# A Mamba block and an FFN on one core: the first stage rebuilt, with TensorE on zeros, softplus in PSUM and masked products for x

## The chip, the cores and the metric

The kernel runs on one core of one Trainium2 chip. A core has a matrix engine (TensorE, PE in the profile; its weight loads are shown as PEld), three elementwise engines (VectorE or DVE, ScalarE or ACT, GpSimd or POOL) and a queue engine (SyncE or SP) that only issues transfers here. They run side by side and wait for one another by semaphores. SBUF is the on-chip memory of 128 partitions; PSUM, also of 128 partitions, receives what TensorE produces, and VectorE and ScalarE can read and write it, too.

The metric is the device time of one execution in microseconds; lower is better. The kernel before has a median of 599.46 us over 3 runs, from 594.8 to 600.17.

## What is computed

Four images of 512 tokens by 256 channels. Everything is float32. A layer norm with a shift and scale per image, an SSM-like attention (Mamba-2 form) with 32 heads of width 8 and state 64, a gated residual, a second layer norm, and an FFN whose hidden layer passes through a Walsh-Hadamard transform:

```python
h = layernorm(x) * (1 + ca) + sa
proj = h @ W_in.T
xBC, z, A_log = split(proj, [4352, 4608])
xBC = causal_conv4(xBC, conv_w) + conv_b
x_, Bm, Cm = split(xBC, [256, 256 + 32 * 64])
a = -softplus(A_log)
Lm = exp(segsum(a))
M = einsum("blhn,bshn,bhls->bhls", Cm, Bm, Lm)
y = einsum("bhls,bshp->blhp", M, x_) + D * x_
x = x + ga * ((y * silu(z + z_bias)) @ W_out.T)
h = layernorm(x) * (1 + cb) + sb
x = x + gb * (fwht(silu(h @ W1.T) * (h @ W3.T)) @ W2.T)
```

The shifts, scales and gates (sa, ca, ga, ...) are slices of silu(c) @ wmod.

## The kernel before

**Tiling.** Eight units, (i, b): i is a half of the heads (16), b an image. A unit has eight pairs of heads, numbered k = 0 to 63 over all units. For a pair, `project` makes the B part (`pbc`, half 0) and the C part (`pcc`, half 1) in PSUM, each with six matmuls (L245): weights and activations are kept as a high and a low float32r half (`split` makes those of the weights: a rounding copy on ScalarE or VectorE, and a subtract on GpSimd), and three of the four products are summed over two halves of the 256 channels. `conv` then applies the four-tap convolution: two operations on ScalarE (L387, L389), two on VectorE (L390, L391) and one on GpSimd (L392). `prep_l` makes the decay matrix of a pair with one bfloat16 matmul of two prepared constants, `dls` and `drs`, into which `load_d` writes the sums of this image from DRAM. `attend` does B times C for two pairs and multiplies with the decays; `turn_b`, `states`, `turn_states`, `intra` and `inter` do the chunked scan of the states, in chunks of 64 tokens.

**The prologue of an image**, in five parts: `normalize` (part 0), `modulate` (part 1: eight transposes into `pt`, then `ht`, the activations in two halves, and `full`), softplus and running sums (part 2: `pa`, abs, exp, ln, max, subtract, scan; then the sums in three bfloat16 `parts`, which go to DRAM in the tiles `p`, `pd` and `pend`), the decays to a chunk's end (part 3) and their transpose `wdec` (part 4).

**The x stage of a unit**: `x_proj` and `conv` give x; `x_part2` copies each chunk twice; `x_part3` transposes it, puts x of each head into its own columns of `xpad` (zero elsewhere), and x times the decays into `xwz` (zero elsewhere).

**Order.** Each piece is traced at a time on an agenda (`at_time`; one unit of time is one pair), with the times in the dict `T`. From that, a planner with its own model of the durations orders the instructions of TensorE, VectorE, ScalarE and GpSimd; only SP's queue keeps the order as written. `behind(engine)` makes an instruction follow a given one on its own engine's queue, without a wait. `AHEAD` is the number of pairs projected before the agenda starts. The start of image 0 is written out by hand (L651 to L688). On PSUM, `m` and `p` are pools of three buffers each.

Of the kernel before, what the change touches and what calls it, by code (L numbers as in the profile page):

```python
# [30 lines left out]
def mamba_ffn(tc, ctx, u, c_t, wmod, win_t, cw, cb, zb, dsk, wo_t, w13_t, w2_t,  # L31
# [50 lines left out]
    ac.activation(warm, neghalf, AF.Tanh)  # L82
    c_sb = cload(c_t.rearrange("(k p) b -> p k b", p=128), [128, 2, NB], "c_sb")
# [15 lines left out]
    wms = {}  # L99
    for grp in (0, 1):  # L100
        load_mod(grp, nc.sync, "bt", 6)
# [45 lines left out]
    xwz = const.tile([128, 4, 4, 2, 2, 16], F32, name="xwz")  # L147
    for t in (xpad, xwz):
        gp.memset(t, 0.0)
# [7 lines left out]
    for t in dls:  # L157
        ac.activation(t, kdl.unsqueeze(1).to_broadcast([94, 8, 128]), AF.Copy)
    for t in drs:
        ac.activation(t, kdr.unsqueeze(1).to_broadcast([94, 4, S]), AF.Copy)  # L160
# [9 lines left out]
    def split(dst, c0, width, ts, e=ac):  # L170

        for k, t in enumerate(ts):
# [5 lines left out]
            gp.tensor_tensor(d[:, 1], t, d[:, 0].bitcast(F32), ALU.subtract)  # L178

    wa = const.tile([128, 2, 32], F32, name="wa")  # L180
    nc.sync.dma_start(wa, win_t[:, 512:544].rearrange("(k p) c -> p k c", p=128))
# [4 lines left out]
    def fetch_quad(n, half, **kw):  # L186
        return fetch(win_t[:, 544 + 1024 * n : 544 + 1024 * n + 1024], 512 * half, 512, f"wq{n}", **kw)

    def split_quad(n, half, ts, e=ac):
        if half == 0:  # L190
            wq[n] = work([128, 2, 2, 1024], f"wq{n}", "wq", 2, F32R)
        split(wq[n], 512 * half, 512, ts, e)
# [4 lines left out]
    def fetch_xz(i, **kw):  # L197
        return fetch(win_t[:, 256 * i : 256 * i + 256], 0, 256, f"wxz{i}", **kw)

    def split_xz(i, ts, e=ac):  # L200
        wxz[i] = work([128, 2, 2, 256], f"wxz{i}", "wxz", 1, F32R)
        split(wxz[i], 0, 256, ts, e)
# [44 lines left out]
    last = {}  # L247

# [10 lines left out]

    def behind(*engines):  # L260
        stack = ExitStack()
        for e in engines:
            stack.enter_context(tc.issue_after(last[e].ins))
        return stack
# [21 lines left out]
    def modulate(b, which, xn):  # L286
# [4 lines left out]
        for t in range(4):  # L291
            for k in range(2):
                pe.transpose(pts[k][:, 128 * t : 128 * t + 128], xn[:, t, 128 * k : 128 * k + 128], ident)  # L293
# [30 lines left out]
    def prologue(b, part, fill=None):  # L324
# [9 lines left out]
        elif part == 2:  # L334
# [8 lines left out]
            at = work([128, 128], f"at{b}", "at", 1)  # L343
            ac.activation(e, pa, AF.Abs)
            last[ve] = ve.tensor_scalar(at, pa, 0.0, -1.0, ALU.max, ALU.mult)
# [4 lines left out]
            ve.tensor_tensor(at, at, e, ALU.subtract)  # L350
            phs = phss[b] = work([128, 128], f"phs{b}", "phs", 1)
            ve.tensor_tensor_scan(phs, reset, at, 0.0, ALU.mult, ALU.add)
# [538 lines left out]
```

## Time and profile before

The profile is of one execution of 600.72 us, whose instructions span 598.8 us; the median of the runs is 599.46 us.

| | us |
|---|---|
| span of the profiled execution | 598.8 |
| its time | 600.72 |
| TensorE busy (matmuls) | 550.4 |
| VectorE busy | 419.3 |
| ScalarE busy | 389.5 |
| GpSimd busy | 329.0 |
| first matmul starts | 7.63 |
| first B part (pbc of pair 0) starts | 15.62 |
| first decay matmul (pl) starts | 28.15 |
| first `xpad` copy, unit 0 | 59.20 |
| first `xpad` copy, unit 1 | 110.71 |
| first `xpad` copy, unit 7 | 427.86 |

Lines of the profile give, for a group, the source line, the engine, the operation, the tile written and those read (with buffer numbers left out), shapes, and the count. In the order of time, the first number is the start, the second the duration, both in us; the bracket at the end is the idle time of that engine before it, and whose end released it. A table by stage has the width first, then the busy time of PE, PEld, DVE, ACT and POOL with the number of instructions, the granted share of the TensorE clock, the DMA engines' busy share, and GB/s.

### The profile page before, as it was taken

The numbers are of one execution on the slowest core, as the hardware profiler recorded it, in microseconds if no ns is written. First come the engines' busy times: TensorE is split into PE (matmuls) and PEld (weight loads), VectorE is DVE, ScalarE is ACT, GpSimd is POOL, SyncE is SP. The second block draws the span as 40 slices with busy tenths as digits, with TensorE's granted clock in tenths as the row PEclk, the third lists the DMA queues.
The fourth block names the chain that finished last, engine by engine and source line by source line (L and its number), as shares of the span: only waits on it lengthen the run. The fifth ranks groups of instructions, "written<-read, shape, count | busy, mean of one in ns | idle before, by whom it ended". The sixth has DMA issues, their size and how long they took to land. (4 is left out here: it accounts for less than half of the span.)

```text
span 598.8 us, 16340 instructions
## 1 busy us (share of the span) xinstructions
PE 550.4 (92%) x6836; PEld 436.1 (73%) x6836; DVE 419.3 (70%) x763; ACT 389.5 (65%) x650; POOL 329.0 (55%) x302
## 2 busy tenths in 40 slices
PE   3798999799899989999999898899989999999996
PEld 3565676577577766767777676667768888888886
DVE  5957987987887785889787778789875354343242
ACT  5879688688956878886794787577774333322321
POOL 5673447255635577556465647466577546334341
PEclk9988999999999999999999799989999999999999
DMA  6323111021122343023103143145138035204021
GB/s 195 117 66 143 36 36 72 21 59 70 42 56 73 112 147 112 3 60 117 59 4 111 67 105 113 58 128 184 38 121 292 22 105 167 99 1 150 1 79 36
DMA packets 42113, 52.00 MB, mean 87 GB/s; under 512 B 18230, under 2 KB 30260, under 8 KB 42040
## 3 DMA queue, kind: packets, MB, share of 16 engines
q1 hardware_dynamic: 40504, 50.54, 26.6%
q8 instruction: 54, 0.88, 0.6%
q10 hardware_dynamic: 1472, 0.38, 0.3%
q14 instruction: 19, 0.16, 0.1%
q0 software_dynamic: 64, 0.05, 0.0%
HBM read 33.51 MB, written 17.44 MB: 85 GB/s over the span
## 5 line engine op out<-in xcount | busy, mean ns | idle before, releaser
L392 POOL TENSOR_TENSOR cc<-cc,cv 128x509 f32<-128x509 f32 x64 | 70.0, 1094 | 70.3 <-DVE cc L391 58.3
L392 POOL TENSOR_TENSOR bc<-bc,cv 128x509 f32<-128x509 f32 x64 | 69.9, 1092 | 56.3 <-DVE bc L391 28.3
L245 PE MATMUL f<-h,wf 128*128 128x512 f32 x384 | 97.2, 394 | 0.0
L245 PEld LDWEIGHTS f<-h,wf 128*128 128x128 f32 x384 | 68.8, 189 | 12.3
L390 DVE SCALAR_TENSOR_TENSOR cc<-pcc,cw_sb,cc 128x511 f32<-128x511 f32 x64 | 47.6, 744 | 35.2 <-ACT cv L389 35.2
L706 POOL TENSOR_TENSOR fl<-ft,fh 128x512 fp32r<-128x512 f32 x31 | 40.0, 1293 | 56.8 <-ACT fh L705 52.2
L387 ACT ACTIVATE bc<-pbc,cb_sb,cw_sb 128x512 f32<-128x512 f32 x64 | 50.0, 781 | 21.1 <-PE pG L258 15.7
L387 ACT ACTIVATE cc<-pcc,cb_sb,cw_sb 128x512 f32<-128x512 f32 x64 | 50.2, 784 | 19.9 <-PE pcc L245 14.8
L245 PE MATMUL pcc<-ht,wq 128*128 128x512 f32 x192 | 55.8, 426 | 7.1 <-DVE dx L489 3.0
L705 ACT ACTIVATE fh<-ft 128x512 fp32r<-128x512 f32 x32 | 20.2, 631 | 58.7 <-DVE ft L702 28.9
L701 DVE SCALAR_TENSOR_TENSOR ft<-ft,f 128x512 f32<-128x512 f32 x32 | 21.9, 687 | 51.3 <-ACT ft L700 51.2
L245 PE MATMUL pbc<-ht,wq 128*128 128x512 f32 x192 | 55.6, 426 | 0.5 <-ACT bt L466 0.5
L245 PE MATMUL pcc<-hr,wq 128*128 128x512 f32 x192 | 54.1, 417 | 1.4 <-DVE bc L391 0.7
L245 PE MATMUL pbc<-hr,wq 128*128 128x512 f32 x192 | 52.0, 405 | 3.3 <-DVE cc L391 3.2
L390 DVE SCALAR_TENSOR_TENSOR bc<-pbc,cw_sb,bc 128x511 f32<-128x511 f32 x64 | 47.5, 743 | 10.7 <-ACT cv L389 10.4
L245 PEld LDWEIGHTS pcc<-ht,wq 128*128 128x128 f32 x192 | 36.9, 201 | 17.0 <-ACT cv L389 3.7
L391 DVE SCALAR_TENSOR_TENSOR bc<-pbc,cw_sb,bc 128x510 f32<-128x510 f32 x64 | 47.6, 743 | 1.3
L391 DVE SCALAR_TENSOR_TENSOR cc<-pcc,cw_sb,cc 128x510 f32<-128x510 f32 x64 | 47.5, 742 | 1.2
L466 ACT ACTIVATE bt<-bT 128x512 f32<-128x512 f32 x64 | 38.7, 605 | 10.8 <-PE bT L464 10.7
L245 PEld LDWEIGHTS pbc<-ht,wq 128*128 128x128 f32 x192 | 37.0, 201 | 10.4 <-ACT bt L466 0.9
L258 PEld LDWEIGHTS pG<-cc,bc 64*64 64x64 f32 x2048 | 34.5, 135 | 13.5 <-issue 7.9
L389 ACT ACTIVATE cv<-pbc,cw_sb 128x512 f32<-128x512 f32 x64 | 44.2, 691 | 0.0
(153 smaller groups left out, 1256.8 us busy)
## 6 DMA issues: line engine op xcount, KB each, us to landing
wq<-win_t SPq DMA_DIRECT2D x16, 256.0 KB
htd<-ht SPq DMA_DIRECT2D x8, 512.0 KB
hr<-htd SPq DMA_DIRECT2D x8, 512.0 KB
h2d<-ht SPq DMA_DIRECT2D x8, 512.0 KB
h<-h2d SPq DMA_DIRECT2D x8, 512.0 KB
x<-u SPq DMA_DIRECT2D x7, 512.0 KB
ex<-pd SPq DMA_DIRECT2D x8, 256.0 KB
ygd<-yg SPq DMA_DIRECT2D x4, 512.0 KB
```

Source lines behind the costliest of these rows:

```text
L245: last[pe] = pe.matmul(ps, w[:, a, k, c0 : c0 + 128], ht[k][:, b], start=(n == 0), stop=(n == 5))
L258: self.before = pe.matmul(*args, **kw)
L387: ac.activation(dst, ps, AF.Identity, bias=cb_sb[:, tl : tl + 1], scale=w[:, 3:4])
L389: last[ac] = ac.activation(v, ps, AF.Copy, scale=w[:, 0:1])
L390: ve.scalar_tensor_tensor(dst[:, 1:], ps[:, : S - 1], w[:, 2:3], dst[:, 1:], ALU.mult, ALU.add)
L391: last["conv"] = ve.scalar_tensor_tensor(dst[:, 2:], ps[:, : S - 2], w[:, 1:2], dst[:, 2:], ALU.mult, ALU.add)
L392: last[gp] = gp.tensor_tensor(dst[:, 3:], dst[:, 3:], v[:, : S - 3], ALU.add)
L466: ac.activation(bts[k], pt, AF.Copy)
L701: ve.scalar_tensor_tensor(t, t, 1.0, p1, ALU.add, ALU.mult)
L705: ac.activation(hi, t, AF.Copy)
L706: (ve if (b, f) == (NB - 1, 7) else gp).tensor_tensor(lo, t, hi.bitcast(F32), ALU.subtract)
```

## The change

- TensorE gets 22 matmuls of zeros at its start and 9 more behind the transposes of image 0.
- The weights that the first stage needs come in one transfer for both halves of the channels instead of two, before the prologue of image 0, into buffers of `ht`; so do the first two groups of `wmod`, into a buffer of `yg`.
- The copies of the constants `dls` and `drs` are halved: the second set is made at time 2.6 of the agenda, behind the last conv then traced on ScalarE.
- `q00` (the weights of pairs 0 and 1) is split after `modulate` of image 0; the low halves of the next weights are made in a given order.
- Softplus: max and add in one operation that writes PSUM in place, and a scan that reads it from there and subtracts.
- The three parts go to DRAM in one transfer (before: four, two of them from GpSimd for image 0), `pd` too.
- Three pairs instead of two are projected before the agenda.
- `xpad` is written by one product with the 0/1 mask `own` for each half of the tokens (before: four copies of 64 partitions), `xwz` by two products of 128 partitions with decays that are zero where they have to be (before: four of 64 partitions). `xwz` has a new layout, `wdec` holds a masked copy for each of two chunks, and `xwz` needs no zeroing any more.
- `dx`'s first column is zeroed on ScalarE instead of VectorE.

```diff
+    def keep_warm(n):
+        for _ in range(n):
+            last[pe] = pe.matmul(warm_ps, idle[:, :128], idle, start=True, stop=True)
+
+    keep_warm(22)
...
+    wm01 = work([128, 2, 2 * DM], "wm01", "yg", 1)
+    nc.sync.dma_start(wm01, wmod[:, : 2 * DM].rearrange("(k p) c -> p k c", p=128))
     for grp in (0, 1):
-        load_mod(grp, nc.sync, "bt", 6)
+        wms[grp] = wm01[:, :, DM * grp : DM * grp + DM]
...
-    for t in (xpad, xwz):
+    for t in (xpad, *sts):
         gp.memset(t, 0.0)
...
-    for t in dls:
-        ac.activation(t, kdl.unsqueeze(1).to_broadcast([94, 8, 128]), AF.Copy)
-    for t in drs:
-        ac.activation(t, kdr.unsqueeze(1).to_broadcast([94, 4, S]), AF.Copy)
+    def spread_constants(n, *engines):
+        with behind(*engines):
+            ac.activation(dls[n], kdl.unsqueeze(1).to_broadcast([94, 8, 128]), AF.Copy)
+            ac.activation(drs[n][:88], kdr[:88].unsqueeze(1).to_broadcast([88, 4, S]), AF.Copy)
+
+    spread_constants(0)
...
+    def fetch_both(src, c0, width, name, tag, bufs):
+        t = work([128, 2, width], f"{name}_{c0}", tag, bufs)
+        nc.sync.dma_start(t, src[:, c0 : c0 + width].rearrange("(k p) c -> p k c", p=128))
+        return [t[:, 0], t[:, 1]]
...
-            last[ve] = ve.tensor_scalar(at, pa, 0.0, -1.0, ALU.max, ALU.mult)
...
-            ve.tensor_tensor(at, at, e, ALU.subtract)
+            ve.scalar_tensor_tensor(pa, pa, 0.0, e, ALU.max, ALU.add)
             phs = phss[b] = work([128, 128], f"phs{b}", "phs", 1)
-            ve.tensor_tensor_scan(phs, reset, at, 0.0, ALU.mult, ALU.add)
+            ve.tensor_tensor_scan(phs, reset, pa, 0.0, ALU.mult, ALU.subtract)
...
-            for t in range(4):
-                (gp if T["p3gp"] and b == 0 and t % 2 else nc.sync).dma_start(p_dr3[b][:, :, 128 * t : 128 * t + 128], parts[32 * t : 32 * t + 32])
+            nc.sync.dma_start(p_dr3[b].rearrange("h r (t l) -> t h r l", t=4), parts)
...
-            wdec[b] = const.tile([128, 4, NH], F32, name=f"wd{b}")
-            ac.activation(wdec[b].rearrange("p t h -> p (t h)"), pw, AF.Copy)
+            wdec[b] = const.tile([128, 4, 2, NH], F32, name=f"wd{b}")
+            for q in range(2):
+                ac.activation(wdec[b][:, :, q], pw.rearrange("p (t h) -> p t h", h=NH), AF.Copy,
+                              scale=own[:, 0, 8 * q : 8 * q + 1])
 
     def write_sums(b, phs):
+        nc.sync.dma_start(p_dr[b].rearrange("h (t l) -> t h l", t=4), phs)
         for t in range(4):
-            nc.sync.dma_start(p_dr[b][:, 128 * t : 128 * t + 128], phs[32 * t : 32 * t + 32])
...
-    AHEAD = 2
+    AHEAD = 3
...
-        ve.memset(de[:, :, 0:1], 0.0)
+        ac.activation(de[:, :, 0:1], de[:, :, 0:1], AF.Copy, scale=0.0)
...
+            v = xpad[:, :, 4 * hf : 4 * hf + 4, :, :16].rearrange("p a c g x -> p a (c g) x")
+            v = bass.AP(v.tensor, v.offset, [v.ap[0], [v.ap[1][0] + 16, 2], *v.ap[2:]])
+            ve.tensor_tensor(v, pt.rearrange("p c (g a x) -> p a (c g) x", g=4, a=2),
+                             own[:, 0].unsqueeze(1).unsqueeze(1).to_broadcast([128, 2, 16, 16]), ALU.mult)
+            for t in range(2):
+                ve.tensor_tensor(xwz[:, 2 * hf + t].rearrange("p h q x -> p q h x"),
+                                 pt[:, 2 * t : 2 * t + 2].rearrange("p q (h x) -> p q h x", x=8),
+                                 wdec[b][:, 2 * hf + t, :, 16 * i : 16 * i + 16]
+                                 .unsqueeze(3).to_broadcast([128, 2, 16, 8]), ALU.mult)
...
-    early = dict(tag="cc", bufs=8)
-    prologue(0, 0)
+    early = dict(get=fetch_both, tag="ht", bufs=6)
     q00 = fetch_quad(0, 0, **early)
-    fxz = fetch_xz(0, **early)
+    nc.sync.dma_start(wa, win_t[:, 512:544].rearrange("(k p) c -> p k c", p=128))
+    fxz = fetch_xz(0, get=fetch_both, tag="cc", bufs=8)
     q01 = fetch_quad(0, 1, **early)
     q10 = fetch_quad(1, 0, **early)
-    q11 = fetch_quad(1, 1)
+    q11 = fetch_quad(1, 1, **early)
+    prologue(0, 0)
+    prologue(0, 1)
+    with behind(ve):
+        split_quad(0, 0, q00, ve)
+    with behind(pe):
+        keep_warm(9)
     with behind(gp):
-        split_quad(0, 0, q00, ve)
-    prologue(0, 1)
-    with behind(gp):
-        for t in sts:
-            gp.memset(t, 0.0)
         gp.tensor_scalar(hzb, zb_sb, 0.5, None, ALU.mult)
...
-            split_xz(0, fxz, ve)
-            split_quad(0, 1, q01, ve)
+            split_xz(0, fxz, ve, True)
+            split_quad(0, 1, q01, ve, True)
+
+            lows.insert(0, lows.pop())
+            for n in range(4):
+                with behind(*[gp] * (n > 0)):
+                    last[gp] = gp.tensor_tensor(*lows.pop(0))
...
-    prologue(0, 3)
+    with behind(ac):
+        prologue(0, 3)
...
+    at_time(2.6, spread_constants, 1, ac)
```

## The prediction

> **What bounds the kernel now.** I read the page first, for shares.
>
> ```profile
> span 598.8 us, 16340 instructions
> PE 550.4 (92%) x6836; PEld 436.1 (73%) x6836; DVE 419.3 (70%) x763; ACT 389.5 (65%) x650; POOL 329.0 (55%) x302
> ```
>
> TensorE leaves 48 us idle in the whole span. A change to the first stage can win that stage's part of the 48 us, plus the time in which TensorE works at half clock. The table by stage shows how much that is:
>
> ```profile
> 0.00:10.00 10.00, 2.37 (x12) 2.40 (x12) 4.26 (x12) 5.15 (x6) 6.42 (x14) 1.00 0.58 165
> 20.00:30.00 10.00, 6.85 (x28) 5.13 (x27) 9.72 (x17) 9.47 (x16) 7.14 (x8) 0.87 0.13 26
> 30.00:45.00 15.00, 13.74 (x115) 9.83 (x113) 8.52 (x20) 11.46 (x21) 10.72 (x10) 0.86 0.22 69
> 75.00:105.00 30.00, 28.96 (x515) 22.52 (x514) 23.87 (x36) 26.63 (x46) 18.31 (x17) 1.00 0.14 54
> ```
>
> (The columns are PE, PEld, DVE, ACT, POOL, granted clock, DMA share, GB/s.) By 75 us TensorE has idled 16.7 us (the stages' busy times summed); from 75 to 105 us it is 97% busy. So time won at the start should be carried on, as far as the other engines follow. The order of time says who sets the start:
>
> ```profile
> 7.63 3.55 PE L111 MATMUL pm<-sc,wm 128*128 128x4 f32 x16 [7.63 <-DMA wm<-wmod]
> 15.62 2.93 PE L245 MATMUL pbc<-ht,wq 128*128 128x512 f32 x6
> 20.72 1.55 PE L245 MATMUL pbc<-ht,wq 128*128 128x512 f32 x6
> 28.15 1.01 PE L428 MATMUL pl<-dr,dl 94*128 94x512 bf16 x2 [3.15 <-DMA dr<-p]
> 29.67 2.91 PE L245 MATMUL pbc<-ht,wq 128*128 128x512 f32 x6
> ```
>
> The same six matmuls take 2.93, 1.55 and 2.91 us. The clock row grants about half at 28 to 34 us; at 15 us it says 1.00, but 0.49 us each is the half-clock pace, so I read it as cold. Then the softplus chain, DVE and POOL:
>
> ```profile
> 18.44 1.37 DVE L350 TENSOR_TENSOR at<-at,spe 128x128 f32<-128x128 f32 x1
> 19.84 1.38 DVE L352 TENSOR_TENSOR_SCAN phs<-reset,at 128x128 f32<-128x128 f32 x1
> 18.20 2.75 POOL L178 TENSOR_TENSOR wq<-wq,wq 128x512 fp32r<-128x512 f32 x2
> 53.89 0.29 DVE L350 TENSOR_TENSOR at<-at,spe 128x128 f32<-128x128 f32 x1 [1.27 <-ACT spe L349]
> ```
>
> With GpSimd busy the subtract takes 1.37 us, ending 0.24 us after GpSimd's own; for image 1, with GpSimd idle, 0.29 us (the scan 0.42). Last, one x stage:
>
> ```profile
> 108.61 1.25 PE L513 MATMUL xt<-ident,xd 128*128 128x128 f32 x8 [1.22 <-DVE l L458]
> 110.71 1.20 DVE L518 COPY xpad<-xt 64x128 f32<-64x128 f32 x4
> 111.92 1.00 DVE L526 TENSOR_TENSOR xwz<-xt,wd 64x128 f32<-64x128 f32 x4
> ```
>
> VectorE has 6.73 us of work in the 7 us from 109 to 116 while TensorE has 5.46: here VectorE decides.
>
> **The change, part by part** (against the profiled execution: span 598.8 us, time 600.72 us, so 1.9 us outside; the median of the runs is 599.46, 1.3 below).
>
> *Warm start.* pm (3.55 us), pt and the first projections run cold. The 22 zeros have no row; their streaming length is the projections', 0.49 us cold and 0.26 warm. TensorE warmed between 14.6 us and about 20.5 (in pcc of pair 0: 2.54 us is about 4.7 slow and 1.3 fast), 5.9 us: 12 cold and 10 warm, 8.5 us from about 1.0. Then pm starts at 9.5 instead of 7.63 and takes half, 1.75: 11.25 against 11.18. If it warms sooner, pm ends at 10. The xn chain ends at 10.50 (unmoved: x halves, rs on GpSimd 1.04 us, four normalises 2.65), so pt ends at 11 to 11.7, not 12.98: 1.3 to 2.0 us won, I take 1.7. The Trainium skill (TensorE: Matmul & The Clock Gate, "What's actually happening") puts the warm-up at about 3.4 us of sustained work in a free-running window; by that, pm would end near 10 and this step win 2.0; the sum below, which goes by a later row, stays.
>
> *Moved split.* Today q00's casts and GpSimd subtracts lie at 10.4 to 14.1, under waits. Now they stand behind the last ht subtract (15.87, less 1.7: 14.2). Casts 2 x 0.43, subtracts 2 x 1.27: low halves exist at about 17.2, and pbc of pair 0, which needs the second low for its fourth term, ends at about 18.0 against 18.55. So only 0.5 of the 1.7 us reaches the first projection, and TensorE half idles for 3 us (the nine zeros lie before it), which can cool it (worth up to 1.4 us on the first pair, a row apart). GpSimd then runs the four lows of wxz and q01 (4.35 us) to 21.5, against 20.95.
>
> *Softplus in PSUM, one p write.* L345 (0.28) goes; the subtract and scan read one operand from PSUM. Without the waits 1.37 and 1.38 become 0.29 and 0.42: 2.0 us. But the four parts operations and df now lie under GpSimd's lows, and those with two SBUF operands can each wait out one, as L350 did (1.1 us each). Net 0.5 to 3.5 us, I take 1.5: parts at 21 instead of 22.47. Four DMAs on two queues (22.50 to 25.45 until dl could issue) become one of SP: one issue 0.66 and the 1.9 us that POOL's queue shows to landing, 2.6 against 2.95. The first pl comes at 26 instead of 28.15. The GPSIMD Engine Reference (1. Specifications) says that GpSimd shares its SBUF interfaces with VectorE, in contention with VectorE instructions of two SBUF inputs or a two-port mode. Row and rule agree that PSUM frees the scan; the same rule speaks against the change at parts and casts, and if by it the chain won nothing and TensorE waited for that, the sum below would be -7.0.
>
> *Third pair ahead.* Pair 2's projections fill 25.0 to 28.15, which was idle (3.15), and run warm: 2.91 + 2.37 - 2 x 1.55 = 2.2. TensorE has done the same work at about 28.5 instead of 34.75: 6.2 us at most. GpSimd, though, has 7 conv adds x 1.09 and 4 lows x 1.26 after 21.5: 34.2 at best for image 1's rs, today at 35.44; VectorE's nm, today 1.15 us late behind a conv (37.63), then comes at once: xn starts near 36.4, not 38.72, 2.3 us. Image 1's pt stands on TensorE around attend(1). So the start gains between 1.2 and 6.2; I take 3.0, near the xn row.
>
> *Constants in two halves.* Today 5.9 us of copies lie in ScalarE's early idle time. The second half, 1.05 + 1.90, moves to time 2.6, that is about 40 us, where ScalarE is busy 11.40 of 12 us (38 to 50) and the pl of pair 4 waits for it. Cost 0 (ScalarE has 4.8 of 15 us free from 60 on) to 2.95: I take 1.5.
>
> *Masked products.* Per half 1.20 + 1.00 = 2.2 us. New: one 128x512 product from PSUM, 0.68 (the row of ot<-po,gate), and two of 256 columns, 0.42 (fo<-pdy,gate): 1.52, less some overlap. About 0.75 saved per half, 12 us of VectorE over 8 units. TensorE idles 1.54 us from 109 to 116, so not all can come back; I take one half's worth per unit, 8 x 0.75 = 6 (bounds 0 and 12).
>
> *Softplus of images 1 to 3.* 0.28 each, and 0.88 and 1.40 instead of 0.29 and 0.42 for images 2 and 3: 4 us of VectorE just before an x stage; half: 2.
>
> *ScalarE extras.* dx's zeroing moves from a 0.07 us memset to ScalarE, 8 x 0.2 (th's row); wd gets a second 0.28, four times: 2.8 us, ScalarE busy 82% in the units: 1 (0 to 2.8).
>
> *At nothing:* the larger loads: all five weight loads and wa now pass SP before image 1's x, wa behind q00 (q00 landed by 12.3, now used at 14; x, wm and q00, 1.5 MB, at the 275 GB/s of 2 to 6 us need 5.5 us; cover some 4 us; wa is wanted at about 13); df's exp, put behind pair 2's and x's convs on ScalarE (some 30 instead of 21.7; pw used it at 34.4; without that cover pw holds TensorE by what is missing); five write_sums DMAs for eight, GpSimd's memsets (2.6 us before 4.45, sts 1.63 for xwz 0.95), states reading xwz in the other layout, 32 columns as before. ScalarE, VectorE, GpSimd and TensorE are ordered anew by the planner from its own model, with no row: either sign, some 3 us.
>
> Sum: -3.0 + 1.5 - 6 - 2 + 1 = -8.5: 600.72 - 8.5 = 592.2, some 591 by the median. I say **592**.
>
> **The rivals.**
> *Wider gain, 585 (22%).* TensorE's own 6.2 us is carried, and the x stage gives 1.2 us a unit: -6.2 + 1.5 - 9.6 - 2 + 1 = -15. For it: TensorE at 97% in 75 to 105. Against it: GpSimd's 12.7 us before rs.
> *Nothing visible, 597.5 (16%).* GpSimd keeps rs where it was (gain 1.2), the constants take 1.5 back, and TensorE, 95% busy between x stages (42.71 of 45 us), absorbs most of VectorE's relief, leaving 3. For it: TensorE's 92%.
> *ScalarE becomes the bound, 605 (17%).* 2.95 + 1.6 + 1.1 = 5.7 us is added to ScalarE on its path, and late convs hold the PSUM buffers that projections want; already TensorE stood still for 2.5 us before pcc at 46.42, while convs were late. It decides if ScalarE's idle time per unit is less than what TensorE saves, so VectorE's relief shows up as VectorE waiting for cv. Against it: cv waits today cost VectorE 46 us in all, but little of the chain. 600.7 + 5.7 - 1.2 = 605.
> *Zeros that do not warm* would be 22 x 0.49 = 10.8 us: pm ends at 15.3, 4 us late, and the start gains nothing (contained in the two cases above).
>
> **How the numbers follow.** A measurement of this kernel tells about 1% (6 us) from no change. The forecast, 45%, spreads over 588 to 597; three quarters of it lie under 593.5 (0.34). Faster: 0.34 + 0.22 = 0.56. Within 1%: 0.11 + 0.16 = 0.27. Slower: 0.17. Range 584 to 603: it leaves out about a third of the wide gain and half of the slow case, under 2 in 10, and takes in both ends of the constants and x stage.
>
> **What would show it.** Right: pm from about 9 us in under 2 us; L350's successor at 0.3 us and the scan at 0.42 beside a busy GpSimd; six-matmul projections at 1.55 us throughout 18 to 28; no 3 us gap before the first pl; xpad plus xwz at 1.4 us a half; the second x stage before 106 us (110.71 today). Wrong: parts operations over 1 us, rs of image 1 after 35, TensorE idle for cv near 45, or an order in the units that leaves x stages later.

## The result and the profile after

The changed kernel takes **603.03 us** (median of 20 runs, 598.62 to 606.6); the kernel before, run beside it, 598.03 (20 runs, 594.8 to 601.72). The ratio is 1.0077, with a 95% interval of 1.005 to 1.0104: slower by 0.8%. The prediction said 592, between 584 and 603. The profiled execution took 601.07 us, 2 us less than its median.

First the shares, from the page of the changed kernel:

```profile
span 599.3 us, 16282 instructions
PE 553.3 (92%) x6867; PEld 434.6 (73%) x6867; DVE 403.5 (67%) x672; ACT 391.2 (65%) x662; POOL 325.9 (54%) x299
```

VectorE lost 15.8 us of work (419.3 before), and the span did not follow. The table by stage of the changed kernel (width, then PE, PEld, DVE, ACT, POOL busy, granted clock, DMA share, GB/s) shows where TensorE lost time instead. The second table is the kernel before in the stages from 45 to 75 us:

```profile
20.00:30.00 10.00, 7.73 (x34) 6.11 (x33) 9.76 (x14) 8.40 (x14) 6.93 (x8) 0.99 0.13 27
30.00:45.00 15.00, 11.15 (x109) 7.96 (x108) 8.06 (x19) 12.72 (x23) 10.31 (x10) 0.89 0.18 48
45.00:60.00 15.00, 10.89 (x114) 7.78 (x112) 8.65 (x18) 14.91 (x25) 5.58 (x6) 0.89 0.37 150
60.00:75.00 15.00, 13.16 (x199) 10.14 (x200) 11.85 (x27) 8.57 (x17) 5.37 (x5) 0.77 0.19 41
```

```profile
45.00:60.00 15.00, 12.49 (x123) 8.98 (x123) 10.96 (x24) 14.12 (x25) 5.83 (x6) 0.89 0.36 140
60.00:75.00 15.00, 14.48 (x215) 10.34 (x213) 13.84 (x36) 10.18 (x19) 6.62 (x6) 1.00 0.18 36
```

From 20 to 30 us it has what was forecast, a warm and busier TensorE (7.73 us for 6.85). From 30 to 75 TensorE is busy for 35.20 us, where before it was 40.71 (13.74 + 12.49 + 14.48), and part of that at a low clock: 0.77 in the last 15 us, 1.00 before. In the order of time, on TensorE of the changed kernel:

```profile
1.17 7.55 PE L98 MATMUL warm<-idle 128*128 128x512 bf16 x22 [1.17 <-DVE idle L93]
8.56 1.84 PE L131 MATMUL pm<-sc,wm 128*128 128x4 f32 x16
...
17.71 1.65 PE L280 MATMUL pbc<-ht,wq 128*128 128x512 f32 x3 [0.32 <-POOL wq L214]
19.16 2.03 PE L280 MATMUL pcc<-ht,wq 128*128 128x512 f32 x6
...
28.89 1.62 PE L280 MATMUL px<-ht,wxz 128*128 128x512 f32 x6 [2.27 <-DVE cc L419]
30.36 0.61 PE L456 MATMUL pl<-dr,dl 94*128 94x512 bf16 x2
...
39.96 0.44 PE L320 MATMUL pt<-ident,xn 128*128 128x128 f32 x2 [3.37 <-ACT xn L310]
...
42.05 1.97 PE L291 MATMUL pG<-cc,bc 64*64 64x64 f32 x60
...
47.67 2.90 PE L280 MATMUL pcc<-ht,wq 128*128 128x512 f32 x6 [2.31 <-ACT dl L180]
```

The zeros warm TensorE: pm takes 1.84 us (3.55 before) and pt starts at 10.26. The gain is then spent: the first projection ends at 19.36 (18.55 before); px waits 2.27 us for a conv, so the gap before the first pl has only moved; TensorE waits 3.37 us for the normalised image 1 before its transposes; and at 45 us it stands still for 2.31 us, as it did for 2.48 before, and works on at half pace. The first decay product on VectorE, at L486, comes at 43.89 us (42.76 before): the rebuilt first stage is 1.1 us later at its end, not 3 us earlier. About half of that is the later start of the transposes (39.96 us for 39.37), and the rest the half clock behind the wait: the 60 matmuls of `pG` take 1.97 us, where they took 1.15. VectorE and GpSimd between:

```profile
18.40 0.28 DVE L376 SCALAR_TENSOR_TENSOR pa<-pa,spe 128x128 f32<-128x128 f32 x1
18.72 0.42 DVE L378 TENSOR_TENSOR_SCAN phs<-reset,pa 128x128 f32<-128x128 f32 x1
19.18 0.74 DVE L382 CAST parts<-phs 128x128 bf16<-128x128 f32 x1
19.84 0.83 DVE L396 TENSOR_TENSOR df<-phs 128x128 f32<-128x128 f32 x1
20.60 0.82 DVE L383 TENSOR_TENSOR rest<-phs,parts 128x128 f32<-128x128 f32 x1
21.45 1.20 DVE L384 CAST parts<-rest 128x128 bf16<-128x128 f32 x1
```

```profile
18.56 1.27 POOL L701 TENSOR_TENSOR wq<-wq,wq 128x512 fp32r<-128x512 f32 x1 [0.38 <-DVE wq L207]
19.79 1.48 POOL L701 TENSOR_TENSOR wxz<-wxz,wxz 128x256 fp32r<-128x256 f32 x2
21.23 1.33 POOL L701 TENSOR_TENSOR wq<-wq,wq 128x512 fp32r<-128x512 f32 x1
...
35.58 2.51 POOL L214 TENSOR_TENSOR wq<-wq,wq 128x512 fp32r<-128x512 f32 x2
38.04 1.03 POOL L302 TENSOR_TENSOR rs<-rs,neghalf 128x4 f32<-128x4 f32 x1
```

Max-and-add takes 0.28 and the scan 0.42 us beside a busy GpSimd, as forecast. But the four operations after them now take 0.74, 0.83, 0.82 and 1.20 us. In the kernel before they took 0.23 to 0.29, two of them in these lines:

```profile
21.26 0.23 DVE L356 CAST parts<-phs 128x128 bf16<-128x128 f32 x1
21.40 0.29 DVE L371 TENSOR_TENSOR df<-phs 128x128 f32<-128x128 f32 x1
```

In the changed kernel all four end with the GpSimd subtracts beside them, as the subtract and the scan did before. The wait went from the scan to its successors, and the parts are done at 22.98 us (22.47 before). The GPSIMD Engine Reference of the Trainium skill (1. Specifications) gives the conditions, two SBUF inputs or a two-port mode of VectorE; these rows agree, and the casts, with one SBUF input, would be of the second kind, which no run here separates.

The x stage is as forecast, a half of it in the time of VectorE's first two rows:

```profile
62.62 0.68 DVE L545 TENSOR_TENSOR xpad<-xt,own 128x512 f32<-128x512 f32 x1
63.22 0.74 DVE L548 TENSOR_TENSOR xwz<-xt,wd 128x256 f32<-128x256 f32 x2
```

1.4 us for 2.2 us. But the first of them starts at 62.62 instead of 59.20, and the second unit's at 117.89 instead of 110.71.

### The profile page after: what moved, and what is told of

It reads as the page before. It is cut to its first block, busy times and chain, and to the rows that moved or that the text cites. A ratio compares the mean times of both kernels' runs of the same rounds, so it can differ in the third digit from the quotient of the medians.

```text
span 599.3 us, 16282 instructions
## 1 busy us (share of the span) xinstructions
PE 553.3 (92%) x6867; PEld 434.6 (73%) x6867; DVE 403.5 (67%) x672; ACT 391.2 (65%) x662; POOL 325.9 (54%) x299
## 4 chain that ended last, share of the span: by engine, by line
PE 59%; ACT 15%; DVE 12%; DMA 6%; issue 3%; POOL 2%; SPq 0%; ACTq 0%; POOLq 0%; DVEq 0%
PE f L280 13%; PE pcc L280 10%; PE pbc L280 7%; PE pdyi L745 4%; PE pdy L745 4%; PE pG L291 4%; ACT cv L417 3%; PE py L574 3%; PE bT L492 3%; PE ps L558 2%; PE po L638 2%; ACT bc L415 2%; PE pz L280 2%; ACT xn L310 2%; DVE cc L418 2%
## 5 line engine op out<-in xcount | busy, mean ns | idle before, releaser
L418 DVE SCALAR_TENSOR_TENSOR cc<-pcc,cw_sb,cc 128x511 f32<-128x511 f32 x64 | 47.5, 743 | 32.4 <-ACT cv L417 32.4
L280 PE MATMUL pcc<-ht,wq 128*128 128x512 f32 x192 | 58.1, 441 | 7.9 <-DVE bc L419 2.9
L418 DVE SCALAR_TENSOR_TENSOR bc<-pbc,cw_sb,bc 128x511 f32<-128x511 f32 x64 | 47.5, 742 | 14.1 <-ACT cv L417 14.0
L280 PE MATMUL pbc<-ht,wq 128*128 128x512 f32 x192 | 53.9, 412 | 2.3 <-POOL wq L214 1.2
L280 PEld LDWEIGHTS pcc<-ht,wq 128*128 128x128 f32 x192 | 38.1, 208 | 20.5 <-DVE bc L419 5.3
L419 DVE SCALAR_TENSOR_TENSOR bc<-pbc,cw_sb,bc 128x510 f32<-128x510 f32 x64 | 47.5, 742 | 1.3
L419 DVE SCALAR_TENSOR_TENSOR cc<-pcc,cw_sb,cc 128x510 f32<-128x510 f32 x64 | 47.5, 742 | 1.1
L486 DVE TENSOR_TENSOR l<-pG,l 128x512 f32<-128x512 f32 x64 | 41.0, 682 | 10.5 <-PE pG L291 6.6
L492 PE MATMUL bT<-ident,bc 128*128 128x128 f32 x256 | 41.2, 283 | 4.2 <-ACT bt L494 2.9
L417 ACT ACTIVATE cv<-pcc,cw_sb 128x512 f32<-128x512 f32 x64 | 44.2, 690 | 1.0 <-POOL bc L420 1.0
```

Of the source, the lines that this page charges most:

```text
L280: last[pe] = pe.matmul(ps, w[:, a, k, c0 : c0 + 128], ht[k][:, b], start=(n == 0), stop=(n == 5))
L417: last[ac] = ac.activation(v, ps, AF.Copy, scale=w[:, 0:1])
L418: ve.scalar_tensor_tensor(dst[:, 1:], ps[:, : S - 1], w[:, 2:3], dst[:, 1:], ALU.mult, ALU.add)
L419: last["conv"] = ve.scalar_tensor_tensor(dst[:, 2:], ps[:, : S - 2], w[:, 1:2], dst[:, 2:], ALU.mult, ALU.add)
L486: ve.tensor_tensor(lts[n], pg, lts[n], ALU.mult)
L492: pe.transpose(pt[:, t], bc[:, 128 * t : 128 * t + 128], ident)
```

## The experiments

The theory after the trace: the masked products win what they should, and three other parts take it back, namely the constants' second half at 46 us on ScalarE, the third pair ahead (its conv adds stand before image 1's rs on GpSimd) and the late split of `q00`. The rival: the change is a loss because the masked products gain nothing, or because the order of the units is worse throughout. All were run in 3 rounds beside the kernel before; a ratio is to that, with its interval. Landmarks are from the profiled executions: "decay product n" is the start of VectorE's multiplication of `pG` by the decays for pair n. Each is one execution, up to 5.6 us away from its kernel's median (591.01 for 596.64 us in the one furthest off), so landmarks tell where a loss lies, and medians how large it is.

**The masked products, alone on the kernel before, and taken out of the changed kernel.**

```diff
-            for pp in range(2):
-                for j in range(2):
...
+            ve.tensor_tensor(v, pt.rearrange("p c (g a x) -> p a (c g) x", g=4, a=2),
+                             own[:, 0].unsqueeze(1).unsqueeze(1).to_broadcast([128, 2, 16, 16]), ALU.mult)
...
```

> The kernel before with the masked products for x alone (xpad, xwz, their layout, wdec, states and turn_states); nothing of the first stage. Theory A (the x stage gives back 0.8 us of VectorE a half, and about half of it comes off the path): 4 to 8 us under the kernel before. Rival (TensorE bounds the units and absorbs it, or the new order of the other engines eats it): within 2 us of the kernel before, with the x stages still 1.4 instead of 2.2 us a half.

Measured: 590.31 us, ratio 0.984 (0.9802 to 0.9878).

> The changed kernel with the four copies and four products per half of before in the x stage (and the old xwz, wdec); first stage as changed. Theory A (units 4 to 7 of the changed kernel win 9 us on the kernel before because of the masked products): that gain goes, the end comes 6 to 10 us after the changed kernel, at about 608. Rival (the 9 us are stalls of the kernel before, behind late transfers and a low clock at 310 to 365 us, that a shifted order avoids): the end within 3 us of the changed kernel.

Measured: 612.54 us, ratio 1.019 (1.0134 to 1.0246). So this part is worth 1.6% (9 us) on the kernel before, and about 1.1% (1.019 less 1.0077, 7 us) within the changed kernel. It does what was asked of it; the rest of the change loses about 2.4%.

**The constants' move.** In the changed kernel the second half goes into ScalarE's wait at 16 us, right behind the ln of image 0; and the reverse, the move alone on the kernel before.

```diff
-            ac.activation(e, e, AF.Ln, bias=1.0)
+            last[ac] = ac.activation(e, e, AF.Ln, bias=1.0)
+            if b == 0:
+                spread_constants(1, ac)
...
-    at_time(2.6, spread_constants, 1, ac)
```

> The changed kernel, but the second half of the constants' copies stands behind the ln of image 0 on ScalarE, where ScalarE waits 3.1 us (16.3 to 19.4), instead of at 46.6 us. Theory A (these 3.0 us on ScalarE delay the convs; TensorE idles 2.3 us before pcc at 47.7, cools and runs the next six matmuls in 2.90 us): pcc starts by 45.5, takes 1.6 us, and every later landmark of units 0 to 2 comes 3 to 5 us earlier than in the changed kernel; the end too, unless it is absorbed. Rival (ScalarE has slack from 60 on, the loss of units 0 to 3 comes from the planner's new order): first decay product of pair 4 at most 1.5 us earlier, end within 1 us of the changed kernel.

Measured: 593.97 us, ratio 0.9916 (0.9883 to 0.9949), 1.6% (9.6 us) less than the changed kernel; decay product 4 at 68.60 instead of 74.66.

```diff
-    for t in dls:
-        ac.activation(t, kdl.unsqueeze(1).to_broadcast([94, 8, 128]), AF.Copy)
-    for t in drs:
-        ac.activation(t, kdr.unsqueeze(1).to_broadcast([94, 4, S]), AF.Copy)
...
+    copies(0)
...
+    at_time(2.6, spread_constants, 1, ac)
```

> The kernel before with only the move of the second half of the constants' copies to time 2.6 of the agenda. Theory A (the move alone delays the convs at 45 us and costs what its removal won in the changed kernel): the first decay product of pair 4 comes 3 to 5 us after the kernel before's 69.4, and the end is 4 to 9 us later. Rival (the move costs only together with the third pair and the late split): within 2 us of the kernel before.

Measured: 606.81 us, ratio 1.0141 (1.0086 to 1.0197). Moving 2.95 us of ScalarE costs 8.4 us here and 9.6 us in the changed kernel. How, TensorE of the kernel before with the move alone shows:

```profile
45.38 2.42 PE L250 MATMUL pcc<-ht,wq 128*128 128x512 f32 x6 [2.15 <-ACT dl L158]
...
58.09 1.09 PE L518 MATMUL xt<-ident,xd 128*128 128x128 f32 x8 [2.17 <-DVE l L463]
60.46 1.08 PE L554 MATMUL py<-l,xpad 128*32 128x64 f32 x32 [1.27 <-DVE xpad L523]
61.88 1.08 PE L538 MATMUL ps<-bt,xwz 128*32 128x128 f32 x16 [0.34 <-DVE xwz L531]
63.02 2.91 PE L250 MATMUL pcc<-ht,wq 128*128 128x512 f32 x6
```

TensorE of the kernel before at the same places:

```profile
46.42 1.74 PE L245 MATMUL pcc<-ht,wq 128*128 128x512 f32 x6 [2.48 <-DVE dx L489]
...
58.75 1.61 PE L245 MATMUL pcc<-ht,wq 128*128 128x512 f32 x6 [0.87 <-DVE bc L391]
60.29 0.65 PE L549 MATMUL py<-l,xpad 128*32 128x64 f32 x32
```

and TensorE of the changed kernel with the constants in the early wait:

```profile
47.57 2.65 PE L280 MATMUL pcc<-ht,wq 128*128 128x512 f32 x6 [1.92 <-DVE bc L421]
...
57.44 1.43 PE L543 MATMUL xt<-ident,xd 128*128 128x128 f32 x8
59.74 1.63 PE L280 MATMUL pcc<-ht,wq 128*128 128x512 f32 x6 [0.88 <-ACT cv L419]
```

The stop at 45 us is in all three (2.15, 2.48 and 1.92): it is not the constants' own. What they add lies 12 us later, at the x stage of unit 0. ScalarE's convs and decays are 1.5 to 2.9 us later than in the kernel before, TensorE stops again for 2.17 and 1.27 us, and then works at half clock: `py` 1.08 us where the kernel before has 0.65, the projection 2.91 instead of 1.61. In slices of 15 us, first of the kernel with the move alone, then of the changed kernel with the constants early:

```profile
60.00:75.00 15.00, 14.20 (x198) 11.07 (x199) 12.86 (x35) 7.12 (x14) 5.32 (x5) 0.79 0.18 38
```

```profile
60.00:75.00 15.00, 14.40 (x218) 10.93 (x218) 14.30 (x29) 11.91 (x23) 7.19 (x7) 1.00 0.26 56
```

TensorE looks as busy (14.20 and 14.40 us), but at 0.79 of the clock instead of 1.00: 15 x 0.21 = 3 us of its work are gone in this slice alone. The delay of one engine was paid twice, as a stop and as the half clock behind it. With the move alone, decay product 2 comes 0.9 us after that of the kernel before, product 4 3.8 and product 8 7.0; at the last one it is 6.8, so the loss lies in the first 100 us. One thing isn't separated: with the copies there, the planner also orders some operations anew. On ScalarE the conv of a C part (52.94 us) now stands ahead of two table loads of image 1's softplus, where it stood behind them (57.13). The runs price the copies and this order together.

**The third pair.** `AHEAD` back to 2, in the changed kernel, and with the constants early too; and `AHEAD = 3` alone on the best kernel below (masked products and zeros).

> The changed kernel with two pairs projected ahead instead of three, all else kept. Theory A (the third pair's two conv adds stand on GpSimd in front of image 1's rs, whose start is what TensorE waits for at 36.6 to 40.0): rs starts at about 36 instead of 38.0, and attend of pair 1 ends 2 us earlier, 42 instead of 44. Rival (the weight lows moved behind image 0's modulate are what makes GpSimd late): rs at 38 again, attend of pair 1 no earlier, and TensorE idle again between px and pl.

Measured: 598.09 us, ratio 0.9977 (0.9944 to 1.001), 1.0% (6 us) less than the changed kernel; rs of image 1 on GpSimd at 35.87 instead of 38.04.

> The kernel with the constants behind the ln, and two pairs projected ahead instead of three. Theory A (the third pair's conv adds delay GpSimd's rs by 2 us whatever the constants do): 2 to 4 us under the kernel with three pairs and the constants behind the ln, rs at 36. Rival (with ScalarE free at 46 us the 2 us at rs are absorbed): within 1.5 us of it.

Measured: 596.29 us (591.2 to 600.6), ratio 0.9948 (0.991 to 0.9987): 2.3 us more than with the constants alone, although decay product 4 comes 1.8 us sooner, at 66.80. Unclear.

> The kernel before with the masked products, 22 zeros, and three pairs projected ahead. Theory A (pair 2's conv adds stand on GpSimd before image 1's rs: the start loses what it wins on TensorE): rs at 37 to 38 instead of 35.5, first decay product 1 to 2 us later than 41.6, end 1 to 5 us over 587. Rival (TensorE's idle 4.5 us before pl, filled, carries on): first decay product earlier than 41, end 2 us under 587.

Measured: 590.5 us, ratio 0.9869 (0.9813 to 0.9925), 3.7 us more than the 586.85 without it. GpSimd of that kernel:

```profile
31.87 1.09 POOL L399 TENSOR_TENSOR bc<-bc,cv 128x509 f32<-128x509 f32 x1
32.91 1.09 POOL L399 TENSOR_TENSOR cc<-cc,cv 128x509 f32<-128x509 f32 x1
...
37.45 1.05 POOL L280 TENSOR_TENSOR rs<-rs,neghalf 128x4 f32<-128x4 f32 x1
```

The third pair's two adds (2.1 us) stand before image 1's rs, which goes from 35.33 to 37.45, and the first decay product from 41.62 to 43.32. That the third pair costs its time by this queue isn't shown, though. The last kernel under "Softplus in PSUM" below has two pairs, the same order at the start and rs at 35.55, and its first decay product comes at 43.35. With two pairs, the two adds stand behind rs, and VectorE's `nm`, the step between rs and xn, runs until both of them are done; with three pairs they are in front. `nm` with two pairs (the kernel below), then with three:

```profile
36.63 2.10 DVE L286 SCALAR_TENSOR_TENSOR nm<-mv,rs 128x4 f32<-128x4 f32 x1 [1.56 <-POOL rs L280]
```

```profile
38.53 0.16 DVE L286 SCALAR_TENSOR_TENSOR nm<-mv,rs 128x4 f32<-128x4 f32 x1 [3.46 <-POOL rs L280]
```

Both end at 38.7 us. And a kernel with its first decay product at 43.25 (softplus in PSUM for image 0, below) still ends at 587.18. So the third pair's price at the end is 6 us, 3.7 and, with the constants early, -2.3, or 3.1 with the split of `q00` early too; where it is paid stays open.

**The split of q00**, back between normalize and modulate (with the constants early):

```diff
+    with behind(gp):
+        split_quad(0, 0, q00, ve)
     prologue(0, 1)
-    with behind(ve):
-        split_quad(0, 0, q00, ve)
```

> The changed kernel with the constants behind the ln and the split of q00 back between normalize and modulate of image 0; the orders of the four engines differ from the constants-behind-ln kernel in this split alone. Theory A (the late split is what gives the start back: GpSimd's lows run under the parts operations and hold them 0.8 to 1.2 us each): pbc of pair 0 ends by 17 instead of 19, parts end by 20.5 instead of 22.9, rs of image 1 at about 36 instead of 38, the end 2 to 4 us earlier. Rival (casts and lows only change places; GpSimd's queue from 20 on is what counts): rs within 1 us of 38, end within 1.5 us.

Measured: 593.97 us (588.8 to 597.0), ratio 0.9909 (0.9875 to 0.9943), the same as without it. The first pbc ends at 16.16 us instead of 19.24, the parts at 21.20 instead of 22.98, the first decay product comes at 42.70 instead of 43.79 (1.1 us sooner), and by decay product 28 only 0.3 us is left. This gain at the start does not reach the end.

**The split of q11 earlier** (agenda 1.15, with the constants early), to bring GpSimd's last lows out of the way of rs:

```diff
-    with behind(gp, ac):
-        split_quad(1, 1, q11)
+    at_time(1.15, split_quad, 1, 1, q11)
```

> As the kernel with the constants behind the ln, and the split of q11 (two copies on ScalarE, two 1.26 us subtracts on GpSimd) moved to time 1.15 of the agenda, so that on GpSimd image 1's rs no longer stands behind it (38.0 us there). Theory A (the start is gated by GpSimd's queue up to rs, then xn and pt; TensorE's earlier end of its projections is lost in the 3.37 us wait before pt at 39.9): rs at 35.5, attend of pair 1 ends at 41.5 instead of 43.9, that wait under 1.5 us, the end some 2 us earlier. Rival (the next limit, ScalarE, is right behind): rs earlier but first decay product within 0.7 us of where it was, end unchanged.

Measured: 596.64 us, ratio 0.9962 (0.9923 to 1.0001). The planner put these subtracts at 17.79 us, ahead of the second low of `q00`; pbc of pair 0 waited 3.11 us for it, and rs came at 39.27, later still. The experiment didn't do what it was made for, and says nothing on the theory.

**The zeros**, 22 at the start, with the masked products, then 1 instead of 22, then alone on the kernel before:

```diff
+    idle = const.tile([128, S], BF16, name="idle")
+    ve.memset(idle, 0.0)
+    warm_ps = ptile("warm")
+    for _ in range(22):
+        pe.matmul(warm_ps, idle[:, :128], idle, start=True, stop=True)
```

> The kernel before with the masked products for x and 22 matmuls of zeros at TensorE's start, no other change; the orders of the other engines are nearly those of the kernel with the masked products alone. Theory A (zeros bring pm, pt and the first projections forward, but GpSimd's rs of image 1 gates the start): pm takes 1.8 instead of 3.5 us, hf starts 1.5 us earlier, but the first decay product moves by under 1 us and the end by under 1.5. Rival (TensorE's time at the start carries): first decay product 1.5 to 3 us earlier, end 2 to 3 us under 590.

Measured: 586.85 us (586.4 to 588.6), ratio 0.9803 (0.9765 to 0.9841), the lowest median here; the interval overlaps that without the zeros (0.9802 to 0.9878). The first decay product comes only 0.16 us sooner than without the zeros, decay product 4 0.18; the 3.5 us to the 590.31 appear from decay product 16 on.

> The kernel before with the masked products and one matmul of zeros instead of 22 (the same tile from the PSUM pool, the same order on every engine). Theory A, the pool's rotation or mere spread makes the late gain of 3.5 us, not the clock: the median lies within 2 us of the 586.9 that 22 zeros gave, though pm is slow again (3.5 us). Rival, the warm clock of the first 12 us makes it: the median lies within 2 us of the 590.3 without zeros.

Measured: 589.01 us, ratio 0.9866 (0.9839 to 0.9894): 2.2 us over 22 zeros, 1.3 under none, with the same order on every engine but for one cast of VectorE at 12 us. By the limits set, that is the rival's side, the warm clock; the intervals still touch those of both neighbours.

> The kernel before with the 22 zeros alone. Theory A, the start alone is worth little: pm takes under 2 us, the first decay product moves by less than 0.7 us, and the median stays within 2 us of before. Rival, the zeros are worth 3.5 us by themselves: the median is 3 to 4 us under before.

Measured: 600.33 us, ratio 1.0036 (1.0012 to 1.006), 2.1 us slower than before. The first decay product comes 0.23 us later. VectorE of this kernel shows why a pt that is ready early is of no use there:

```profile
12.39 0.43 DVE L182 CAST wq<-wq 128x512 fp32r<-128x512 f32 x1 [1.38 <-DMA wq<-win_t]
...
13.07 1.61 DVE L303 TENSOR_SCALAR hf<-pt,msc 128x512 f32<-128x512 f32 x2
```

The second cast of `q00` stands ahead of `hf` and waits for its weights, so `hf` starts at 13.07 us (13.02 before). In the changed kernel, where the casts come later, it starts at 11.37. With the masked products the order of the start is the same, so the gain there (3.5 us, not clear of noise) has another cause than an earlier start, if it is one; which stays open.

**Small parts**, on the kernel with masked products and zeros: `dx` zeroed on ScalarE, and the one-transfer writes of p and pd.

> The kernel before with the masked products, 22 zeros, and dx's first column zeroed on ScalarE instead of VectorE. Theory A (eight times 0.26 us on a busy ScalarE, and a step that dc waits for, cost something in the units): 1.5 to 4 us over 587. Rival (it frees VectorE of a stall and costs nothing): within 1 us of 587, or under it.

Measured: 587.54 us, ratio 0.9821 (0.9768 to 0.9874). Eight more operations on ScalarE cost nothing that can be seen.

```diff
-            for t in range(4):
-                (gp if T["p3gp"] and b == 0 and t % 2 else nc.sync).dma_start(p_dr3[b][:, :, 128 * t : 128 * t + 128], parts[32 * t : 32 * t + 32])
+            nc.sync.dma_start(p_dr3[b].rearrange("h r (t l) -> t h r l", t=4), parts)
...
```

> The kernel before with the masked products, 22 zeros, and the parts and pd in one transfer each. Theory A (one transfer of 384 pieces takes as long to land as the four together): dl issues within 0.5 us of 25.5, pl within 0.5 us of 28.2, end within 1.5 us of 587. Rival (freed SP and GpSimd time carries): pl 1 us or more earlier, end 1.5 to 4 us under 587.

Measured: 589.82 us, ratio 0.986 (0.9798 to 0.9922). That is 3 us more than with four transfers, by intervals that overlap: no gain, and the end outside both theories. In the changed kernel, SP's queue shows the write and the first load that waits for it:

```profile
23.01 0.67 SPq L389 DMA_DIRECT2D p<-parts  x1
26.20 0.34 SPq L449 DMA_DIRECT2D dl<-p  x1
```

3.19 us for one transfer; four on two queues took 2.95 (22.50 to 25.45).

**Softplus in PSUM**, on the kernel with masked products and zeros: for all images, for image 0 alone, for images 1 to 3 alone.

```diff
-            last[ve] = ve.tensor_scalar(at, pa, 0.0, -1.0, ALU.max, ALU.mult)
...
-            ve.tensor_tensor(at, at, e, ALU.subtract)
+            ve.scalar_tensor_tensor(pa, pa, 0.0, e, ALU.max, ALU.add)
...
-            ve.tensor_tensor_scan(phs, reset, at, 0.0, ALU.mult, ALU.add)
+            ve.tensor_tensor_scan(phs, reset, pa, 0.0, ALU.mult, ALU.subtract)
```

> The kernel before with the masked products, 22 zeros and softplus in PSUM (max and add in one operation, the scan from PSUM). Theory A, it wins at the start what the forecast took from it and no more than 1.5 us reaches the end: the first decay product comes 0.5 to 1.5 us earlier than the 41.62 without it, the median 0 to 2 us under 586.9. Rival, the parts operations wait under GpSimd's low halves, so that nothing is won: the first decay product within 0.4 us, the median 587 to 590.

Measured: 594.88 us, ratio 0.9946 (0.9917 to 0.9976), **8 us slower** than without it. Both theories fell. The parts end at 21.39 us instead of 22.36, VectorE's first conv starts as before (22.23 and 22.28, it waits for ScalarE), and the first decay product comes 0.43 us later. The loss begins at decay product 12 (+1.9) and is 9.2 us by product 28.

> The kernel before with masked products, 22 zeros, and softplus in PSUM for image 0 alone; the planner's order in the units is then that without it. Theory A, the 8 us that softplus in PSUM cost came from the order of the units from 105 us on, which the planner makes anew when images 1 to 3 are shortened: the median is 585 to 589. Rival, the shorter chain of image 0 itself brings the loss (its parts end 1 us sooner, something downstream collides): 593 to 597.

Measured: 587.18 us, ratio 0.9837 (0.9782 to 0.9893).

> The same, but softplus in PSUM for images 1 to 3 alone: the start is that of the kernel without it, the order of the units that of softplus for all images. Theory A, the order decides: the first decay product at 41.6, 4 to 5 us late at product 16, the median 593 to 597. Rival, the order costs nothing: 585 to 589.

Measured: 593.2 us, ratio 0.9913 (0.9879 to 0.9946); late by 5.8 us at product 16 (1.7 of it from the start) and by 9 at 28. The medians are 6.4 us apart. So the first stage is not the main cause: when images 1 to 3 are shortened, the planner orders the units anew from 105 us on, and that order is worse. ScalarE, for one, now runs `zt`, `zz` and `xn` (from 117.92 us on) ahead of a conv and of the `bt` that TensorE then waits for; without it that conv stands ahead of all three (115.79). TensorE of the kernel with softplus in PSUM for images 1 to 3:

```profile
124.04 0.63 PE L480 MATMUL bT<-ident,bc 128*128 128x128 f32 x4 [0.85 <-ACT bt L482]
125.37 0.44 PE L444 MATMUL pl<-dr,dl 94*128 94x512 bf16 x1 [0.71 <-DVE sn L574]
126.02 2.93 PE L250 MATMUL pcc<-ht,wq 128*128 128x512 f32 x6 [0.21 <-DVE bc L407]
```

Three short stops, 1.8 us in all, and then a projection at 2.93 us, half clock; from 120 to 135 us the clock is 0.89, and TensorE busy for 13.23 us of 15. In the same window of the kernel without it, TensorE is busy for all of it, at full clock:

```profile
120.00:135.00 15.00, 15.00 (x266) 11.91 (x264) 12.11 (x17) 13.48 (x24) 8.27 (x8) 1.00 0.15 27
```

That it is images 1 to 3, and not the start, was shown by the two halves. That it is their order is read from these stops, which name other operations than softplus; which of the swaps does it was not tried. A rival stays untested: softplus now holds its PSUM buffer `pa` until the scan has read it. The one stop of TensorE there that names the scan is 0.32 us (at 104.8).

**All three faults undone in the changed kernel** (constants early, two pairs ahead, q00 split early):

> The changed kernel with its three suspected faults undone together: the constants' second half in ScalarE's early wait, two pairs ahead instead of three, q00 split between normalize and modulate. Theory A, the account by parts adds up (603 less 9 for the constants, 4 for the third pair, 0 to 1 for the split): 588 to 592. Rival, the single prices overlap, since one late start is filled by what another leaves: 593 to 597, no better than the constants' move undone alone.

Measured: 590.86 us (585.6 to 592.0), ratio 0.9875 (0.9825 to 0.9926), 2.0% (12 us) less than the changed kernel, for 9.6, 4 to 6 and 0 by the single runs: by these, the account closes within 4 us. The steps to it don't add up as well: with the constants early, two pairs made it 2.3 us slower and the early split 0, and both together 3.1 us faster. What is left of the change then (masked products, zeros, softplus, the loads) is worth 1.25%, no more than the masked products alone (1.6%) or with the zeros (2.0%).

## Why the prediction was wrong

**Right.** pm in 1.84 us from 8.56, so that it ended at 10.40 (11.25 by the prediction's row, near 10 by the page's 3.4 us; the zeros stayed at half pace for some 5.2), and hf 1.65 us sooner (11.37 for 13.02; 1.7 was said); max-and-add and scan at 0.28 and 0.42 beside GpSimd; projections at 1.52 us from 21, though not from 18 (2.03 for the second); the x stage at 1.4 us a half. Three of its signs for "wrong" came too: a parts operation over 1 us (1.20), rs of image 1 after 35 (38.04), x stages later in the units.

**"Constants in two halves ... Cost 0 to 2.95: I take 1.5"** is the step that failed most: 8.4 us on the kernel before, 9.6 in the changed one. The upper end was the length of the copies on ScalarE, as if the path could lose no more than the engine was held. The runs show a second price: TensorE's stops at 58 to 61 us and the half clock behind them, which takes 3 us of work from one slice. The planner's new order around the copies, which the prediction put at nothing, is part of the measured price, with a share that stays open.

**"So the start gains between 1.2 and 6.2; I take 3.0"** became a loss of 1.1 us at the first decay product. Its base was that GpSimd could run its seven conv adds and four lows from 21.5 us on, "34.2 at best for image 1's rs". The adds wait for VectorE's conv products, and VectorE was in the parts until 22.98; the first add began at 24.57, and 24.57 + 7 x 1.09 + 4 x 1.26 + 1.1 of gaps between the adds is 38.3, near the 38.04 seen (some of them overlap). The third pair's two adds are part of it, by 2.2 us (rs at 35.87 without them); what that does at the end stays open. "Parts at 21" failed by the rule that the prediction named as speaking against the change: the waits moved on to casts and df. "2.6 against 2.95" for the one write was 3.19. And "low halves exist at about 17.2" held (17.66), but pbc of pair 0 took three stretches with waits and a cooled clock: it ended at 19.36, not 18.0.

**"Masked products ... 6"**: right in the mechanism, mis-sized; 7 to 9.6 us. Each half saved what was said (0.8 us), and 0.9 to 1.2 us a unit came back, where the prediction took 0.75 of the 1.5 saved.

**"Softplus of images 1 to 3 ... 2"** and **"ordered anew by the planner ... either sign, some 3 us"** at nothing: the second decided, with 6 to 8 us of loss on the kernel where it was isolated, as far as the stops there tell. In the changed kernel its own share was not isolated; the three faults undone leave room for 2 to 4 us of it (0.9875 for 0.984 and 0.9803).

**"ScalarE extras ... 1"**: dx cost nothing, and with the masked products (which bring wd's copies) the time still fell by 9 us. The rival at 605 came nearest in the number, but not by its mechanism. It spread 5.7 us of ScalarE over all units and decided by VectorE waiting for cv; those waits, 46 us before, are 46 after (32.4 and 14.0). The largest loss came at one place.

The sum with the measured terms: -7 to -9.6 masked products, +8.4 to 9.6 constants, -2.3 to +6 third pair. That is anything from -3.5 to +8.6, with nothing for the rest of the start and the softplus, which weren't measured in the changed kernel. The +4.6 measured (0.77% of 598) lies in it; of its terms only the first two are sure in sign. The distance from the prediction's -8.5 is 7 to 8 us by the constants (8.4 to 9.6 for 1.5) and 4 by the start, at its end (1.1 lost for 3.0 won).

## What to carry to other kernels

Work moved out of an engine's idle time onto a busy stretch is not priced by its length: ask which engine stops for it, and whether that stop lets TensorE's clock fall. Here a wait that was removed from one operation passed to the next ones beside the same busy engine, so price the whole chain until the other engine is done. And where a planner orders the instructions, shortening one operation elsewhere can cost more than it saves; hold the order fixed, or run each part alone, before giving its gain to the sum.

## What the runs showed of the hardware

The spread between executions of one kernel follows TensorE's granted clock: over 79 runs of the kernel before, from 593.96 us at a mean clock of 0.991 to 602.76 at 0.973, the two are correlated at -0.90, with 3.8 us for each 0.01. What makes the clock fall in one execution and not in another was not traced.

In these traces a stretch at half the granted clock, behind the cold start, lasts 3.4 or 6.8 us, but for those that the kernel's end cuts off: 47.5 to 50.9 and 61.1 to 68.0 us in the changed kernel, for example. Such a stretch needed no long stop: 1.9 to 2.5 us before a projection were followed by 2.42 to 2.90 us for six matmuls (1.5 warm) or, in the kernel before, by one at 1.74 and a second at 2.76, and 1.8 us in three pieces was enough as well. That the fall comes now at once and now one projection later agrees with the free-running window of the Trainium skill (TensorE: Matmul & The Clock Gate, "What's actually happening"). That page puts the window at some 3.4 us and lets the clock fall after at least one idle window; all these stops were shorter, so here the rows decide.

The same 22 zeros took 7.55 us in the changed kernel, 7.87 alone on the kernel before, and 6.38 with the masked products: the clock comes at a different point of the row each time. Some 12, 14 and 7 of them took 0.43 us each and the others 0.22, so by an estimate from these TensorE warmed within 5.2, 6.0 and 3.0 us. The prediction's 12 cold ones were right for the changed kernel by luck; its 8.5 us came from lengths that were too long, 0.49 and 0.26.
